# Zeros beside the last part's sums, attention products and sums one step behind the scores, and another order of the network steps

## The chip, the cores and the metric

The kernel runs on one core of a Trainium2 chip. The metric is device time in microseconds (us) of one execution, the median of several runs. A profile of one execution stands beside them: every instruction of the engines, and the transfers. TensorE is PE in it (its weight loads PEld), VectorE DVE, ScalarE ACT, GpSimd POOL, SyncE SP. PE, DVE and ACT compute; POOL issues the gathers here; SP issues most other transfers. Each engine works through its own instructions in order, and waits on semaphores for the others.

## The reference

Four layers over 3125 nodes of 256 features and 50000 edges sorted by destination, each added to `x` after a layer norm:

```python
# 1: relational graph layer, 16 relations
transformed = jnp.einsum('ni,rio->rno', h, weight)
out = segment_sum(transformed[rel_type, src] * norm, dst)
# 2: 16 experts, top 2, silu(x w1) * (x w2), then w3
# 3: two attention layers over the same edges, 8 heads of 32
h = (x @ W).reshape(N, HEADS, HEAD_DIM)
e = leaky_relu(alpha_s[src] + alpha_d[dst], 0.2)
ex = jnp.exp(e - segment_max(e, dst)[dst])
alpha = ex / (segment_sum(ex, dst)[dst] + 1e-16)
out = segment_sum(h[src] * alpha[:, :, None], dst) + b
# 4: a shared network of three layers, plus 4 expert networks of three
#    layers, the best 2 of them weighted by a softmax over their gates
return shared + gated
```

The first attention layer ends in an elu and feeds the second.

## The kernel before

Nodes lie in 25 tiles of 125 (`T` tiles of `R` rows), `x` in `xr`. The kernel goes through its stages one after the other.

**The relational layer.** `half_of_table` (L1251) multiplies half of the 16 weight matrices with one tile of normalized nodes (PE, L1266), copies the product to the buffer `tr` (ACT, L1269; two buffers) and writes 1 MB to a table in DRAM (SP, L1273). The loop over `n` runs 50 such halves. Between them stand the other engines' work in a written order: the layer norms of the next tiles (DVE and ACT, L104), edge records (n = 2), their placing into source order (`placing`, n = 10 and 11), the sending of places (`sending`, from n = 12), and from `n == 2 * S0[1]` on the gathers of table rows by the edges (POOL, L113) and their sums by destination (PE, L985, with one-hot matrices from DVE). Source nodes are in three parts (`S0 = (0, 7, 15)`), so that sums of the first two parts run while later halves are made; `a0`, `a1` set how fast `part_summed` is taken. The records for placing go out to `recs` and come back through loads that POOL issues (L1079).

**The last part's sums and the routing.** The loop over `items` (25 of them, one per tile) gathers and sums the third part, finishes a tile, and makes its expert logits. `blank` (L1356) fills the slots `xs` of the experts' inputs with zeros, 1 MB at a time from a row of zeros in SBUF, eleven transfers on SP in all; later the nodes are scattered into these slots by POOL. `blank` depends on nothing but the zeros. The loop's order on PE, DVE, ACT and SP is written by hand (`manual_schedule`), while what the zeros of `xs` wait for leaves them free to be issued earlier.

**The experts** (`pieces`): slots of 256 rows, PE-bound, and then the way back to the nodes.

**The attention layers.** `layer` (L1908) runs steps s = −1 to 25 with four tiles in hand: `new` (s+1), `now` (s), `old` (s−1), `older` (s−2). For a tile, `fetch` gathers 17 rows of 128 edges into three buffers `g0`, `g1`, `g2` (6, 6 and 5 chunks; three buffers each), `scans` finds running maxima (DVE L1824, L1825, after ACT's copies L1821), `one_hot` makes the destination matrix `oh` (DVE L1837), `carried` joins maxima over partitions (DVE L1842 to L1848, PE L1851), `lookup` and `destinations` bring the destination's term (PE L1880, DVE L1833), `scores` makes `z = exp(...)` (DVE, ACT L1866), `weighted` multiplies each gathered row by `z` (DVE L1886, one call for each of the three parts), `summed` adds up by destination (PE L1894) and `means` divides (DVE L1900 to L1906). Before, `weighted(now, 0..2)` and `summed(now, 0..1)` stand in the tile's own step, after its scores, and `summed(old, 2)` in the next. `tail1` to `tail4` are what follows `means`: for layer 1 the elu, a transpose, the product with the next layer's weights and the write of the next table.

A gather into a buffer waits for the sum that last read it:

```python
                    if len(added[k]) >= 3:
                        after_all(rows[0], [added[k][-3]])
```

**The networks** run inside layer 2, on pairs of tiles. `residual` is layer 2's `tail1`; `normalize`, `first_layers`, `gates`, `second_layers`, `choice`, `shares`, `spread`, `shared_out`, `third_layers` and `finish` are called from three places in a step, each with a lag in steps from the pair's second `residual` (`due`); a lag that is even falls on even steps and an odd one on odd steps:

```python
            def slot(s):
                run(s, (1, first_layers), (2, second_layers), (2, spread), (4, third_layers))
            def mid(s):
                run(s, (4, finish), (1, gates))
            def end(s):
                run(s, (2, shared_out), (0, normalize), (1, choice), (1, shares))
```

`slot` stands after `scores`, `mid` and `end` at the end of the step. `last` does the remaining pairs after the last step. `sel` and `sel_lt`, two small constants of the networks, are set up by POOL's iota (L2052) and DVE (L2054 to L2056); in the trace this work lies in layer 1.

Of the kernel before, what the change touches and what calls it, by code (L numbers as in the profile page):

```python
# [17 lines left out]
T = 25  # L18
# [5 lines left out]
H = 8  # L24
# [21 lines left out]
def gnn_kernel(ctx: ExitStack, tc: tile.TileContext, a: dict, out: bass.AP):  # L46
# [834 lines left out]
    def by_tiles(ctx, start_i, hard):  # L881
# [120 lines left out]
        with ExitStack() as mk:  # L1002
# [279 lines left out]
            with tc.manual_schedule():  # L1282
# [5 lines left out]
                for t in range(T):  # L1288
                    for half in range(2):
# [16 lines left out]
                        if n == 2:  # L1306
                            edge_records(sp, *loaded)
                            short.close()
                            sp = short.enter_context(tc.tile_pool(name="places_t", bufs=1))
                            placing = places(sp, *edges_of_tiles(sp))  # L1310
                        elif n == 10:
                            take_one(placing)
                        elif n == 11:
                            take_one(placing)
                            take_one(placing)
                            short.close()
                            sp = short.enter_context(tc.tile_pool(name="sent_t", bufs=1))
                            sending = sent(sp)
                        elif n > 11:
                            take_one(sending)  # L1320
                            take_one(sending)

                        if n == 2 * S0[1]:
                            for r in rels[:3]:
                                for k in range(2):
                                    fetch(r, k)
                                    if r.n == 0:
                                        hot(r, k)
                        a0, a1 = 2 * S0[1] + 1, 2 * S0[2] + 1
# [18 lines left out]
        with ExitStack() as st:  # L1348
# [7 lines left out]
            def blank(k, c0, c1):  # L1356

                nc.sync.dma_start(xs[k][c0 * SL:c1 * SL, :].rearrange("(p a) f -> p a f", p=128),
                                  zero[:, None, :].to_broadcast([128, (c1 - c0) * SL // 128, D]))
# [348 lines left out]
            with tc.manual_schedule(engines={ET.PE, ET.DVE, ET.Activation, ET.SP}):  # L1708
                slot_steps = pieces()
                route = routing(batches[0])  # L1710
                for s, w in enumerate(items):
                    if 1 <= s < 12:
                        k, c = (0, 4 * (s - 1)) if s < 6 else (1, 4 * (s - 6))
                        blank(k, c, min(c + 4, USED[k]))
# [47 lines left out]
        with ExitStack() as st:  # L1762
# [4 lines left out]
            fx = fixed.tile([128, 128 + D], F32, name="fx")  # L1767
            iota_ps, bias_ps = fx[:, :R], fx[:R, 128:]
            nc.vector.tensor_copy(iota_ps, iota_r[:, :R])
# [3 lines left out]
            def hidden(wx, xT):  # L1773
                p = ps.tile([R, D + 2 * H], F32, name="p_x")
                for k in range(2):
                    nc.tensor.matmul(p, xT[:, k, :], wx[:, k, :], start=(k == 0), stop=(k == 1))  # L1776
                return p
# [18 lines left out]
            def fetch(w):  # L1796
                w.g = []
                for k, (i0, i1) in enumerate(PARTS):
                    g = pool.tile([128, i1 - i0, DX], F32, name=f"g{k}", bufs=3)
                    rows = [gather(g[:, i - i0, :], w.h_tab, src_i[:, w.t, i:i + 1]) for i in range(i0, i1)]  # L1800

                    if len(added[k]) >= 3:
                        after_all(rows[0], [added[k][-3]])
                    w.g.append(g)
# [48 lines left out]
            def scores(w):  # L1853
# [11 lines left out]
                w.z = ad_e.rearrange("q h i -> q (h i)").rearrange("q (i h) -> q i h", h=H)  # L1865
# [22 lines left out]
            def summed(w, k):  # L1888

                if k == 0:  # L1890
                    w.p = ps.tile([R, DX], F32, name="p_sum")
# [16 lines left out]
            def layer(h_tab, ad, bias, tail1, tail2, tail3, tail4, slot=None, mid=None, end=None, last=None):  # L1908
# [7 lines left out]
                for s in range(-1, T + 1):  # L1916
# [9 lines left out]

                    if now:
                        one_hot(now)
                        destinations(now)
                    if older and s < T:  # L1930
                        tail4(older)
                    if now:
                        carried(now)
                    if old:
                        summed(old, 2)
# [6 lines left out]
                    if now:  # L1942
                        weighted(now, 0)
                    if old:
                        means(old)
                        tail1(old)
                        tail2(old)
                        tail3(old)
                    if now:
                        summed(now, 0)  # L1950
                        weighted(now, 1)
                        summed(now, 1)
                        weighted(now, 2)
                    if s == T:
                        tail4(older)
                        tail4(old)
                    if mid and now:
                        mid(s)
# [5 lines left out]
            def transposed(x):  # L1964
                p = ps.tile([128, 2, R], F32, name="p_x")
# [120 lines left out]

            def first_layers(u):
                n = u.n * R
                xT = pool.tile([128, 2, 2 * R], F32, name="xT2", bufs=2)
                for i in range(u.n):  # L2090
                    nc.scalar.copy(xT[:, :, i * R:(i + 1) * R], transposed(u.xc[:, i, :]))
                u.h1 = pool.tile([128, 2, 2 * R], F32, name="sh1")
                u.g1 = pool.tile([128, n_e, 2 * R], F32, name="eh1")
                for w, dst, bias in ([(s1[:, :, m * 128:(m + 1) * 128], u.h1[:, m, :n], b1[:, m:m + 1])
                                      for m in range(2)] +
                                     [(e1[:, e], u.g1[:, e, :n], eb1[:, e:e + 1]) for e in range(n_e)]):
                    p = ps.tile([128, 2 * R], F32, name="p_x")
                    for k in range(2):
                        nc.tensor.matmul(p[:, :n], w[:, k, :], xT[:, k, :n], start=(k == 0), stop=(k == 1))  # L2099
                    relu(dst, p[:, :n], bias)  # L2100
                u.pg = ps.tile([R, 2, n_e], F32, name="p_x")
# [14 lines left out]
            def second_layers(u):  # L2116
# [3 lines left out]
                p = ps.tile([128, 2 * R], F32, name="p_x")  # L2120
                for k in range(2):
                    nc.tensor.matmul(p[:, :n], s2[:, k, :], u.h1[:, k, :n], start=(k == 0), stop=(k == 1))
                relu(u.h2[:, :n], p[:, :n], b2)
                for half in range(2):
                    p = ps.tile([128, 2 * R], F32, name="p_x")
                    for k in range(2):
                        nc.tensor.matmul(p[:, :n], e2[:, 2 * half + k, :], u.g1[:, 2 * half + k, :n],
                                         start=(k == 0), stop=(k == 1))
                    relu(u.g2[:, half, :n], p[:, :n], eb2[:, half:half + 1])
# [44 lines left out]
            def spread(u):  # L2174
                n = u.n * R
                p = ps.tile([n_e + 1, 2 * R], F32, name="p_x")
# [4 lines left out]
                u.pw = ps.tile([128, 2, 2 * R], F32, name="p_x")  # L2181
# [7 lines left out]
            def third_layers(u):  # L2189
                u.po = ps.tile([R, 2, D], F32, name="p_x")  # L2190
# [21 lines left out]

            def slot(s):
                run(s, (1, first_layers), (2, second_layers), (2, spread), (4, third_layers))

            def mid(s):
                run(s, (4, finish), (1, gates))

            def end(s):
                run(s, (2, shared_out), (0, normalize), (1, choice), (1, shares))  # L2220

            def last():

                u, v, w = pairs[-3:]
                for step, p in ((third_layers, u), (finish, u), (first_layers, v), (normalize, w), (gates, v),
                                (second_layers, v), (choice, v), (shares, v), (first_layers, w), (gates, w),
# [5 lines left out]
            with tc.manual_schedule():  # L2232
                layer(tabs[1], ads[1], biases[1], residual, *[lambda w: None] * 3, slot, mid, end, last)
# [43 lines left out]
```

## Time and profile before

Seven runs took 2641.51 us in the median (2630.93 to 2648.55). The profiled execution took 2639.61 us, of which the span of the instructions is 2637.9.

| stage | from | to (us of the span) |
|---|---|---|
| relational table, sums of two parts | 0 | 670 |
| last part's sums, routing, scatters | 670 | 830 |
| experts, way back | 830 | 1433 |
| attention layer 1 (gathers 1433.6 to 1970.0) | 1433 | 1970 |
| hand-over | 1970 | 2014 |
| attention layer 2 and networks (gathers 2013.7 to 2548.9) | 2014 | 2549 |
| after the last gather | 2549 | 2638 |

The page gives busy time, share of the span and instructions of each engine, and the span in 40 slices of some 66 us. A digit is the busy share of a slice in tenths; `PEclk` is the clock granted to TensorE in tenths of full speed, and `DMA` the busy share of the 16 transfer engines:

```profile
PE 1964.2 (74%) x8604; PEld 1432.9 (54%) x8604; DVE 1370.0 (52%) x2950; ACT 800.3 (30%) x1699; POOL 1399.5 (53%) x1445
...
PE   5667879999564999997975266656653578888888
...
DVE  4068863322451441132114477777763687877783
...
POOL 1106555775677704120015777777763777777740
PEclk9788989999776999998995588888876788999898
DMA  6524434554336747674534555555552554444430
```

The first slice shows transfers at six tenths, POOL at one tenth and DVE at four; PE is near full in the middle of the table and in the experts (slices 13 to 20), and POOL at seven tenths through the attention layers, where the time between two gathers is not counted as busy.

A line of the profile's groups names line, engine, operation, `out<-in` and the number of instructions, then busy time and mean ns of one, then idle time before them with what ended it. A wait reads "engine tile line <- what it waited for: us in total, times, longest". In a timeline a row is start, length, engine, line, operation, shapes and the count of instructions in the group, and in brackets the idle time before it and its releaser.

### The profile page before, as it was taken

The page shows a single profiled execution, that of the slowest core. Times are in us where ns is not written, and L with a number is a line of the kernel's source. Part 1 is how long each engine was busy: PE and PEld are TensorE (multiplying, and loading weights), DVE is VectorE, ACT ScalarE, POOL GpSimd, SP SyncE. Part 2 cuts the span into 40 slices and gives each one's busy share as a digit, 9 for nine tenths or more (in the row PEclk, how much of TensorE's full clock was granted, in tenths as well). Part 3 has the DMA queues.
Part 4 walks back from the last instruction along what each step waited for, and adds up shares of the span by engine and source line. Part 5 has one row for each costly group of instructions (what it writes and reads, how often), then busy time and mean ns, then how long its engine had stood idle before and what let it go on. Part 6 is the DMA issues. An engine that isn't in the chain of part 4 may idle for free.

```text
span 2637.9 us, 26960 instructions
## 1 busy us (share of the span) xinstructions
PE 1964.2 (74%) x8604; PEld 1432.9 (54%) x8604; DVE 1370.0 (52%) x2950; ACT 800.3 (30%) x1699; POOL 1399.5 (53%) x1445
## 2 busy tenths in 40 slices
PE   5667879999564999997975266656653578888888
PEld 2234545555443878886862144444442466666665
DVE  4068863322451441132114477777763687877783
ACT  2221112222021242242223233333331344454542
POOL 1106555775677704120015777777763777777740
PEclk9788989999776999998995588888876788999898
DMA  6524434554336747674534555555552554444430
GB/s 215 207 96 141 135 117 162 200 190 167 106 104 196 232 127 249 197 213 135 192 108 114 151 139 144 146 139 140 139 138 53 136 131 138 140 136 141 135 92 15
DMA packets 192309, 386.35 MB, mean 146 GB/s; under 512 B 39900, under 2 KB 112588, under 8 KB 186659
## 3 DMA queue, kind: packets, MB, share of 16 engines
q0 software_dynamic: 76464, 189.38, 26.7%
q1 hardware_dynamic: 104543, 184.41, 20.6%
q10 hardware_dynamic: 11152, 10.75, 1.2%
q8 instruction: 71, 1.16, 0.2%
q14 instruction: 79, 0.65, 0.1%
HBM read 294.45 MB, written 89.87 MB: 146 GB/s over the span
## 4 chain that ended last, share of the span: by engine, by line
PE 48%; DVE 17%; DMA 10%; POOL 10%; issue 9%; ACT 5%; SPq 0%; ACTq 0%; POOLq 0%; DVEq 0%
PE ph L1574 10%; PE p_tr L1266 9%; POOL g L113 9%; PE p_sum L1894 7%; PE sum L985 5%; PE py L1584 5%; DMA table_t<-tr 4%; PE p_x L2099 3%; DMA g<-h_tab_t,src_t 2%; DVE oh L1837 2%; DMA g<-table_t,rg_t 2%; DVE g L1886 2%; PE p_x L2196 2%; PE p_x L1776 1%; DVE to_lane L1165 1%
## 5 line engine op out<-in xcount | busy, mean ns | idle before, releaser
L113 POOL DMA_INDIRECT g<-h_tab_t,src_t x850 | 810.5, 954 | 323.4 <-issue 266.7
L113 POOL DMA_INDIRECT g<-table_t,rg_t x450 | 448.4, 996 | 339.6 <-issue 115.5
L1894 PE MATMUL p_sum<-g,oh 128*125 128x264 f32 x1700 | 472.1, 439 | 14.3 <-DVE g L1886 11.7
L1894 PEld LDWEIGHTS p_sum<-g,oh 128*125 128x125 f32 x1700 | 362.0, 217 | 98.1 <-DVE g L1886 12.1
L1266 PE MATMUL p_tr<-w_rel_t,xT_t 128*125 128x512 f32 x800 | 371.7, 619 | 43.2 <-ACT tr L1269 43.2
L1574 PE MATMUL ph<-xcT,w 128*128 128x256 f32 x1312 | 310.1, 384 | 0.7 <-ACT xcT L1566 0.7
L985 PE MATMUL sum<-g,oh 128*125 128x256 f32 x900 | 243.1, 423 | 63.3 <-DMA g<-table_t,rg_t 33.1
L1266 PEld LDWEIGHTS p_tr<-w_rel_t,xT_t 128*125 128x125 f32 x800 | 155.7, 197 | 233.0 <-issue 177.2
L1886 DVE TENSOR_TENSOR g<-g,p_e 128x1536 f32<-128x1536 f32 x150 | 244.9, 1661 | 47.0 <-ACT g L1868 28.3
L1574 PEld LDWEIGHTS ph<-xcT,w 128*128 128x128 f32 x1312 | 248.9, 193 | 34.2 <-ACT xcT L1566 1.1
L1578 DVE TENSOR_TENSOR hT<-silu,ph 128x256 f32<-128x256 f32 x164 | 68.8, 421 | 376.7 <-ACT silu L1577 376.6
L1269 ACT COPY tr<-p_tr 125x512 f32<-125x512 f32 x200 | 115.2, 587 | 486.9 <-PE p_tr L1266 400.2
L985 PEld LDWEIGHTS sum<-g,oh 128*125 128x125 f32 x900 | 184.6, 210 | 111.7 <-issue 56.5
L113 POOL DMA_INDIRECT y<-ys,pos_i x50 | 61.4, 1228 | 327.3 <-DMA ys<-yc 297.6
L1000 DVE TENSOR_TENSOR xr<-xr,sum 125x256 f32<-125x256 f32 x75 | 31.4, 418 | 245.4 <-PE sum L985 202.3
L1584 PE MATMUL py<-w,hT 128*128 128x256 f32 x656 | 155.4, 380 | 0.2 <-DVE hT L1578 0.2
L1577 ACT ACTIVATE silu<-ph 128x256 f32<-128x256 f32 x164 | 62.9, 384 | 237.0 <-PE ph L1574 236.9
L1584 PEld LDWEIGHTS py<-w,hT 128*128 128x128 f32 x656 | 123.6, 190 | 16.9 <-DVE hT L1578 0.6
L1967 PE MATMUL p_x<-ident,en 125*128 125x125 f32 x50 | 16.7, 436 | 143.9 <-DVE en L1996 143.9
L1837 DVE TENSOR_TENSOR oh<-lo_t,fx 128x2125 f32<-128x2125 f32 x50 | 117.2, 2343 | 0.0
L1873 ACT ACTIVATE rows<-rows,minus_p 125x2176 bf16<-125x2176 bf16 x50 | 105.2, 2105 | 26.3 <-DMA g<-h_tab_t,src_t 17.7
L1866 ACT ACTIVATE p_e<-es 128x136 f32<-128x136 f32 x50 | 14.4, 287 | 322.4 <-DVE es L1864 322.4
(341 smaller groups left out, 2473.9 us busy)
## 6 DMA issues: line engine op xcount, KB each, us to landing
w<-in_L_ffn_w SPq DMA_DIRECT2D x123, 512.0 KB
table_t<-tr SPq DMA_DIRECT2D x44, 1000.0 KB
rows<-lo_rows_t SPq DMA_DIRECT2D x50, 531.2 KB
g<-h_tab_t,src_t POOLq DMA_INDIRECT x850, 2.9
xc<-xs_t SPq DMA_DIRECT2D x41, 256.0 KB
ys<-yc ACTq DMA_DIRECT2D x41, 256.0 KB
xs_t<-zero SPq DMA_DIRECT2D x9, 1024.0 KB
g<-table_t,rg_t POOLq DMA_INDIRECT x450, 5.5
```

The lines of the kernel that those rows point to most:

```text
L113: return nc.gpsimd.indirect_dma_start(out=dst, out_offset=None, in_=table, in_offset=bass.IndirectOffsetOnAxis(ap=idx, axis=0))
L985: m = nc.tensor.matmul(r.p[:R, :D], r.oh[k][:, i - i0, :], r.g[k][:, i - i0, :], start=(i == r.parts[0][0]), stop=(i == r.parts[1][1] - 1))
L1266: m = nc.tensor.matmul(p, xT[:, k, t * R:(t + 1) * R], w_rel[:, k, r0:r0 + 2, :].rearrange("p r o -> p (r o)"), start=(k == 0), stop=(k == 1))
L1269: nc.scalar.copy(tr[:, 2 * q * D:(2 * q + 2) * D], p)
L1574: nc.tensor.matmul(p[:, which, :], u.w12[:, which, k, m * 128:(m + 1) * 128], u.xcT[:, k, :], start=(k == 0), stop=(k == 1))
L1578: nc.vector.tensor_mul(u.hT[:, m, :], s, p[:, 1, :])
L1584: nc.tensor.matmul(u.py[:, j, :], u.hT[:, m, j * 128:(j + 1) * 128], u.w3[:, m, :], start=(m == 0), stop=(m == nh - 1))
L1837: nc.vector.tensor_tensor(w.oh, lo[:, w.t, :, None].to_broadcast([128, CT, R]), iota_ps[:, None, :].to_broadcast([128, CT, R]), OP.is_equal)
L1873: nc.scalar.activation(w.rows, w.rows, AF.Abs, bias=minus_p[:R, :])
L1886: nc.vector.tensor_mul(g, g, w.z[:, i0:i1, :, None].to_broadcast([128, i1 - i0, H, HD]))
L1894: m = nc.tensor.matmul(w.p, w.oh[:, i, :], w.g[k][:, i - i0, :], start=(i == 0), stop=(i == CT - 1))
L2099: nc.tensor.matmul(p[:, :n], w[:, k, :], xT[:, k, :n], start=(k == 0), stop=(k == 1))
```

## The change

Three things move, and two layouts go with them. The zeros each wait for the last sum so far, so they can't be issued before the last part's sums, and begin at item 0 instead of 1. In the relational loop the placing, the sending and the first gathers stand one half or two later. In the attention layers `weighted` and `summed` of a tile move to the next step, between the `one_hot` of the tile that follows and its scores; `tail3` comes to the front of a step, `destinations` behind the sums, `tail4` behind `tail1`. The networks' steps are called from the front (`early`), before the scores (`fill`), after them (`slot`) and at the end; `turned`, the two transposes of a pair, becomes a step of its own.

```diff
-                        elif n == 10:
+                        elif n == 11:
                             take_one(placing)
-                        elif n == 11:
+                        elif n == 12:
...
-                        elif n > 11:
+                        elif n > 12:
...
-                        if n == 2 * S0[1]:
+                        if n == 2 * S0[1] + 2:
...
-                        a0, a1 = 2 * S0[1] + 1, 2 * S0[2] + 1
+                        a0, a1 = 2 * S0[1] + 2, 2 * S0[2] + 1
...
-                nc.sync.dma_start(xs[k][c0 * SL:c1 * SL, :].rearrange("(p a) f -> p a f", p=128),
-                                  zero[:, None, :].to_broadcast([128, (c1 - c0) * SL // 128, D]))
+                fill = nc.sync.dma_start(xs[k][c0 * SL:c1 * SL, :].rearrange("(p a) f -> p a f", p=128),
+                                         zero[:, None, :].to_broadcast([128, (c1 - c0) * SL // 128, D]))
+                after_all(fill, [sums_of[-1]])
...
-                    if 1 <= s < 12:
-                        k, c = (0, 4 * (s - 1)) if s < 6 else (1, 4 * (s - 6))
+                    if s < 11:
+                        k, c = (0, 4 * s) if s < 5 else (1, 4 * (s - 5))
```

In the attention layers, the layout in PSUM (`fx` holds the row numbers in bf16, the bias and now `z`; `p_x` has three banks and `p_sum` one) and the step:

```diff
-            fx = fixed.tile([128, 128 + D], F32, name="fx")
-            iota_ps, bias_ps = fx[:, :R], fx[:R, 128:]
-            nc.vector.tensor_copy(iota_ps, iota_r[:, :R])
+            fx = fixed.tile([128, 64 + D + CT * H], F32, name="fx")
+            iota_ps, bias_ps = fx[:, :64].bitcast(BF16)[:, :R], fx[:R, 64:64 + D]
+            z_ps = fx[:, 64 + D:].rearrange("q (i h) -> q i h", h=H)
...
-                    if len(added[k]) >= 3:
-                        after_all(rows[0], [added[k][-3]])
+                    if w.t >= 3:
+                        after_all(rows[0], [added[k][w.t - 3]])
...
+                    if older:
+                        tail3(older)
+                    if early:
+                        early(s)
                     if now:
                         one_hot(now)
-                        destinations(now)
-                    if older and s < T:
-                        tail4(older)
+                    if old:
+                        weighted(old, 0)
+                        summed(old, 0)
                     if now:
                         carried(now)
                     if old:
-                        summed(old, 2)
+                        for k in (1, 2):
+                            weighted(old, k)
+                            summed(old, k)
+                    if now:
+                        destinations(now)
+                    if fill:
+                        fill(s)
                     if new:
                         lookup(new)
                     if now:
                         scores(now)
                     if slot and now:
                         slot(s)
-                    if now:
-                        weighted(now, 0)
                     if old:
                         means(old)
                         tail1(old)
+                    if older:
+                        tail4(older)
+                    if old:
                         tail2(old)
+                    if s == T:
                         tail3(old)
-                    if now:
-                        summed(now, 0)
-                        weighted(now, 1)
-                        summed(now, 1)
-                        weighted(now, 2)
-                    if s == T:
-                        tail4(older)
                         tail4(old)
-                    if mid and now:
-                        mid(s)
                     if end and now:
                         end(s)
```

And the networks, where `first_layers` and `second_layers` also put two products into one tile of PSUM before the activations read them:

```diff
+            def turned(u):
+                n = u.n * R
+                p = ps.tile([128, 2, 2 * R], F32, name="p_x", bufs=3)
+                for i in range(u.n):
+                    for k in range(2):
+                        nc.tensor.transpose(p[:, k, i * R:(i + 1) * R], u.xc[:, i, k * 128:(k + 1) * 128], ident[:R, :R])
+                u.xT = pool.tile([128, 2, 2 * R], F32, name="xT2", bufs=2)
+                nc.scalar.copy(u.xT[:, :, :n], p[:, :, :n])
...
+            def early(s):
+                run(s, (2, gates), (3, shared_out), (5, finish), (1, turned), (2, second_layers), (4, third_layers))
+
+            def fill(s):
+                run(s, (2, choice), (2, shares))
+
             def slot(s):
-                run(s, (1, first_layers), (2, second_layers), (2, spread), (4, third_layers))
-
-            def mid(s):
-                run(s, (4, finish), (1, gates))
+                run(s, (1, first_layers), (2, spread))
 
             def end(s):
-                run(s, (2, shared_out), (0, normalize), (1, choice), (1, shares))
+                run(s, (0, normalize))
```

`last` calls `turned` ahead of each of its two `first_layers`; the rest of it is as before.

## The prediction

> **What bounds the kernel now.** I read the page first, then busy times by stage, then the waits of the two stretches that the change touches, then the chain and single rows in layer 2.
>
> ```profile
> span 2637.9 us, 26960 instructions
> ...
> q10 hardware_dynamic: 11152, 10.75, 1.2%
> ...
> xs_t<-zero SPq DMA_DIRECT2D x9, 1024.0 KB
> ```
>
> The zeros are 10.75 MB on a queue of their own. The next view gives, for a stretch, its length, the busy time of PE, PEld, DVE, ACT and POOL, the granted clock, the DMA share and GB/s.
>
> ```profile
> 20.00:55.00 35.00, 23.40 (x58) 9.93 (x57) 25.17 (x49) 9.61 (x23) 2.99 (x8) 0.90 0.69 232
> 55.00:116.00 61.00, 31.43 (x60) 12.56 (x59) 4.10 (x6) 10.15 (x24) 14.29 (x26) 0.75 0.62 214
> 116.00:160.00 44.00, 28.80 (x69) 13.01 (x67) 10.29 (x18) 10.33 (x24) 0.00 (x0) 0.81 0.32 127
> ...
> 670.00:830.00 160.00, 74.55 (x256) 56.51 (x256) 53.30 (x140) 22.82 (x62) 122.03 (x123) 0.69 0.39 111
> ...
> 1433.00:1970.00 537.00, 298.34 (x1483) 225.21 (x1483) 359.19 (x704) 175.28 (x334) 406.90 (x426) 0.79 0.56 144
> ```
>
> No engine is full between 20 and 160; the transfers are (214 to 232 GB/s). In 670 to 830 and in layer 1 the bound is POOL, which issues gathers back to back (a gather each 1.25 us, 17 per tile: 21.3 us). Waits of 20 to 150:
>
> ```profile
> DVE ln_st L104 <- ACT ln_sq L103: 96.3, 3, 67.6
> ACT tr L1269 <- DMA table_t<-tr: 78.6, 9, 16.2
> ```
>
> ACT waits 78.6 us for table writes to free `tr`, and VectorE's normalization waits behind it on ACT. In layer 2 the chain of waits names PE and DVE in turn; one odd and one even step of it:
>
> ```profile
> 2412.47 2.34 DVE oh L1837
> ...
> 2417.00 3.91 PE p_sum L1894 x10
> 2420.91 0.41 PE p_ad L1880 x17
> 2421.63 0.65 ACT xT L2091 x2
> 2422.32 5.34 PE p_x L2099 x24
> ...
> 2439.28 3.51 PE p_sum L1894 x10
> 2442.80 0.45 PE p_ad L1880 x17
> 2443.24 1.32 PE p_x L2122 x4
> 2444.56 1.70 PE p_x L2127 x8
> ...
> 2448.15 4.24 PE p_x L2196 x16
> 2452.41 0.69 DVE xr L2200
> ```
>
> The scan L1824 starts at 2411.64, 2433.97 and 2455.69: steps of 22.33 and 21.72. From tile 27 (2079.55) to tile 49 (2566.72) there are 22 steps, 487.2 us, 22.14 each, against POOL's 21.3: the lag behind the last gather grows from 2.2 to 17.9 us. So layer 2 is set by this PE/DVE/ACT loop, not by POOL.
>
> **The change, part by part.** The profiled execution took 2639.61 (span plus 1.7), 1.9 below the median of the runs; the sum starts there.
>
> *Zeros, and the placing one half later.* Half 1's last copy L1269 ends at 25.9, half 10's at 146.5: nine halves in 120.6, 13.4 each. Without zeros a half costs (write + filling)/2 with its two buffers. A write takes 13.3 to 16 in the later halves; filling is four copies spaced by their eight matmuls, about 4: 8.7 to 10, I take 9.1. Half 10 then ends at 25.9 + 82 = 108. The records for placing are loaded by POOL (L1079, 59.8 to 101.9, landing 5.6 later), so placing cannot start before 107.5; it started at 150.35, and I expect 113: −37 (−31 to −42). From there to n=25 a half takes some 15 us of VectorE, then PE sets the pace (108 of 112 us busy in 448 to 560). Placing from n=11 instead of 10 means that one more half lies done in the time that transfers set, and one fewer (6.9 us) in PE's: −7 (−8 to 0). Together **−44** (−50 to −31) at the first gather of part 3 (670.7).
>
> The eleven fills now wait on SP, each for the last sum of the item before it. Behind them on SP stand the slot and weight loads (791), needed after the last fill. They run beside part 3's gathers: 105 GB/s plus 1 MB per item of 8.7 us (120 GB/s) is 225, and the stretch 20 to 55 shows 232. So nearly all fits: **+3** (0 to +15, the upper end if landing slips by 1.3 us in each of the eleven).
>
> [...]
>
> *Layer 1: products and sums one step later.* L1886 and L1894 of a tile move into the next step. Busy DVE work per step is 359/25 = 14.4, PE 12: POOL stays the bound. But the buffers of tile 3 come free one step later. At 1481.7 DVE stood 18.7 us at L2054, which waits for POOL's iota queued behind 51 gathers; its step resumed at 1500.3. POOL's gathers of tile 3 begin at 1500.2; they would now wait for tile 0's products and sums in that late step, some 9 us (one_hot 2.33, product 1.75, sums 3.9). **+8** (0 if the iota lands elsewhere, +10). The hand-over to layer 2 has the same work, with one tile's sums more behind the last scores: **+2** (−2 to +8).
>
> *Layer 2, odd step* (`turned`, `shared_out`, `finish` at the front; `first_layers` late), from the scan: scans .83, `shared_out` .66, `finish` .60, `one_hot` 2.26 (start to start), the product of part 0 1.6: 5.95. PE has then been idle over 3 us, and the sums start. What idling costs is seen here:
>
> ```profile
> 2549.59 0.38 PE L1851 MATMUL p_c<-ident,cin 8*128 8x8 f32 x2 [2.22 <-DVE cin L1847]
> ...
> 2549.90 4.06 PE L1894 MATMUL p_sum<-g,oh 128*125 128x264 f32 x10
> ...
> 2541.23 5.61 PE L1894 MATMUL p_sum<-g,oh 128*125 128x264 f32 x24
> ```
>
> Ten matmuls after 2.22 us of idling took 406 ns each; 24 without idling 234 each. The twelve of part 0 so take 4.6 to 4.9, I take 4.6; the transposes .3, parts 1 and 2 2.8 and 2.3 at 234 ns: 16.0. Lookup .6, `first_layers` 24 × .21 = 5.0: 21.7. Its last activations .9, the residual's two ACT passes 1.06, the copies L1821 .6: the next scan at **24.3**, 22.5 if PE stays fast. ACT works in order, so those copies stand behind all six activations; before, L1886 and `choice` filled DVE there.
>
> [...]
>
> *Even step* (`gates`, `second_layers`, `third_layers` at the front, `choice` and `shares` in the middle, `normalize` late). DVE is the loop: scans .83, `gates` .37, `one_hot` 2.26, the products 1.6 + 1.57 + 1.4, `carried` 1.41, the reduction L1833 .49, `choice` and `shares` 4.15, `scores` 3.08, `means` 1.34, the residual 1.09: 19.6, each from start to start in before's rows. Then comes what two products (3.15) and PE hid before: residual's ACT 1.06, the table load 1.28, square root .2, reciprocal and scaling 1.2, copies .6: 4.3. Next scan at **23.9**.
>
> A pair of steps is 48.2 against 44.28 (2 × 22.14): +3.95. The first pair of tiles has no networks behind it yet, so ten pairs: **+40** (+21 with fast PE, +50 with a microsecond more in each odd step). The wider `p_x` (three banks) and `first_layers` by twos save nothing: its 24 matmuls are PE-bound (5.34). The one-hot against a bf16 row in PSUM costs the same (its rows: 1.1 ns an element in either form). Table loads stay 12 and 12.
>
> *After the last scan*: the last sums and `choice` stand before the rest: **+3** (0 to +6).
>
> Sum: −44 + 3 + 8 + 2 + 40 + 3 = **+12**: 2651.6, by the median's 1.9 **2653**.
>
> **Rivals.**
> *A, the other side: the zeros' gain stays whole and layer 2 stays fast.* If PE's matmuls hold 234 ns in odd steps, layer 2 costs +21, and if POOL's iota is passed, layer 1 costs 0: −44 + 3 + 0 + 2 + 21 + 3 = −15: **2627**. It decides from a layer 2 step of 23.2 or less (then its +23 less 44 wins). For it: the 24-matmul rows; against: every ten-matmul row after a PE wait.
> *B, the zeros bound nothing.* If table writes land no faster (ACT's waits stay) or the records' loads slip, the gain is 20: 2653 + 24 = **2677**. For it: 127 GB/s with still 4 to 6 us waits in 116 to 160 after the last zero.
> *C, the loop falls under POOL's pace.* DVE's own work is some 19 us a step. If `normalize` and the activations hide, layer 2 takes 21.3 a step: 22 × .84 = −18 in place of +40: **2595**. Against it: ACT in order before L1821.
> *D, zeros collide with the gathers*, +15 for +3: **2665**.
>
> **How the numbers follow.** Forecast .50, A .20, B .12, C .10, D .08. About 0.3% (8 us) can be told from no change: 2633.6 to 2649.4. The forecast gives slower .40, same .10; A faster .16, same .04; B slower .12; C faster .10; D slower .08. Faster .26, same .14, slower .60. The forecast's own range is 2636 to 2672; to hold 8 in 10 with A, D and most of B: 2615 to 2682 (C is left out).
>
> **What would show it.** After: the rows `xs_t<-zero` near 625 to 725; ACT's wait for table writes halved; placing near 113 and part 3's first gather near 627. Gathers of tile 3 waiting for sums of PE. Scans of layer 2 spaced 24.3 and 23.9, the twelve first sums above .35 us each, POOL waiting for sums near the end. I am wrong if the scans are spaced 21.4 (C), or part 3 starts after 645 (B).

## The result and the profile after

The changed kernel takes 2662.6 us in the median of 18 runs, the kernel before 2638.3 in 46 runs beside them: a ratio of 1.0091 (95% interval 1.0079 to 1.0103), slower by 24 us. Forecast were 2653 us, slower, in a range of 2615 to 2682; that was 12 us above the 2641.5 of the kernel before that the forecast started from, so the direction came true and the measured step is twice as large. The profiled execution's span went from 2637.9 to 2656.9. From the first gather of each stage in the two traces:

| stretch | before | after | difference | forecast |
|---|---|---|---|---|
| start to part 3's first gather | 670.72 | 645.06 | −25.7 | −44 |
| to layer 1's first gather (1433.61, 1410.84) | 762.9 | 765.8 | +2.9 | +3 |
| to layer 2's first gather (2013.71, 1993.14) | 580.1 | 582.3 | +2.2 | +10 |
| to the scan of tile 27 (2079.55, 2059.06) | 65.8 | 65.9 | +0.1 | 0 |
| 22 steps to the scan of tile 49 (2566.72, 2582.01) | 487.2 | 523.0 | +35.8 | +40 |
| to the end of the span | 71.2 | 74.9 | +3.7 | +3 |
| sum | 2637.9 | 2656.9 | +19.0 | +12 |

The stretches of the front, in the same columns as before (length; busy time of PE, PEld, DVE, ACT, POOL; clock; DMA share; GB/s):

```profile
20.00:55.00 35.00, 25.24 (x58) 10.86 (x57) 25.14 (x49) 9.45 (x23) 3.72 (x9) 0.85 0.45 154
55.00:116.00 61.00, 53.88 (x125) 22.72 (x124) 4.10 (x6) 20.16 (x47) 14.32 (x26) 0.97 0.39 146
...
670.00:830.00 160.00, 83.03 (x329) 67.26 (x328) 59.13 (x150) 29.86 (x78) 122.41 (x124) 0.74 0.63 197
```

Between 55 and 116 PE does 125 matmuls where it did 60; the zeros are gone from there. They are now issued from 638.1 to 737.9; between 670 and 830, 111 GB/s became 197, and POOL's busy time is the same 122.4 us (122.0). ACT's wait for the table writes, from 20 to 150:

```profile
DVE ln_st L104 <- ACT ln_sq L103: 63.0, 3, 47.9
ACT tr L1269 <- DMA table_t<-tr: 48.2, 10, 9.8
```

78.6 us of waiting are 48.2 now, and none of these waits is above 9.8. In layer 2 the chain of waits over an odd step and the beginning of an even one:

```profile
2415.27 0.63 DVE eh L2206
2415.90 0.60 DVE xr L2219
2416.50 2.28 DVE oh L1841
2418.78 1.67 DVE g L1890
2420.49 4.93 PE p_sum L1898 x12
2425.42 0.22 PE p_c L1855 x2
2425.64 5.09 PE p_sum L1898 x22
2430.73 0.41 PE p_ad L1884 x17
2431.14 5.19 PE p_x L2116 x24
2436.36 0.83 ACT eh L2093 x2
2437.19 0.40 ACT ln_xc L2081
2438.20 0.43 ACT es L1825 x2
2438.66 0.45 DVE fw L1828
```

The scans start at 2414.42, 2438.66 and 2462.20: 24.24 for the odd step, 23.54 for the even one. This is one serial chain: DVE makes `oh` and the first product, PE sums all 34 matmuls, looks up, and does the first layers, and ACT's last activations and the residual come before the three copies that the next scan needs. The timeline has the twelve slow sums, the wait of VectorE at the odd step's end, and the uncovered normalization at the even one's:

```profile
2420.49 4.93 PE L1898 MATMUL p_sum<-g,oh 128*125 128x264 f32 x12 [3.45 <-DVE g L1890]
...
2438.66 0.44 DVE L1828 TENSOR_TENSOR_SCAN fw<-cut_ft,es 128x136 f32<-128x136 bf16 x1 [5.40 <-ACT es L1825]
...
2446.71 2.94 PE L1898 MATMUL p_sum<-g,oh 128*125 128x264 f32 x12
...
2459.02 1.28 ACT L2087 ACT_TABLE_LOAD   x1
...
2460.55 0.17 DVE L2088 RECIPROCAL ln_st<-ln_st 125x2 f32<-125x2 f32 x1 [1.35 <-ACT ln_st L2087]
2460.75 0.91 ACT L2090 ACTIVATE ln_xc<-ln_xc,ln_st 125x256 f32<-125x256 f32 x2 [0.23 <-DVE ln_st L2088]
2461.57 0.60 ACT L1825 COPY es<-g 128x48 f32<-128x48 f32 x3
```

The same twelve sums take 4.93 us after PE idled 3.45 us, and 2.94 in the even step, where the second and third layers keep PE busy ahead of them, from 2439.24 on. The granted clock (the figure behind POOL's count) shows what differs:

```profile
2407.50:2410.91 3.41, 1.42 (x10) 0.69 (x6) 2.37 (x8) 1.61 (x7) 2.68 (x3) 1.00 0.39 104
2410.91:2424.56 13.65, 6.11 (x17) 4.13 (x18) 10.41 (x14) 8.99 (x13) 9.74 (x11) 0.50 0.56 139
2424.56:2458.69 34.13, 30.68 (x172) 24.13 (x170) 23.67 (x66) 11.60 (x30) 22.80 (x24) 1.00 0.45 121
```

Nearly all of the slow sums lie in a stretch at half clock (0.50, 13.65 us long), the even step's in one at full clock (1.00, 34.13 us). The half clock begins 9.6 us ahead of the first slow sum, behind 3.41 us in which PE still worked 1.42 us.

### The profile page after: what moved, and what is told of

The parts are those of the page before. It is cut to its first block, busy times and chain, and to the rows that moved or that the text cites. A ratio compares the mean times of both kernels' runs of the same rounds, so it can differ in the third digit from the quotient of the medians.

```text
span 2656.9 us, 27198 instructions
## 1 busy us (share of the span) xinstructions
PE 1976.5 (74%) x8608; PEld 1435.8 (54%) x8608; DVE 1362.7 (51%) x2951; ACT 787.0 (30%) x1688; POOL 1402.8 (53%) x1445
## 5 line engine op out<-in xcount | busy, mean ns | idle before, releaser
L1890 DVE TENSOR_TENSOR g<-g,fx 128x1536 f32<-128x1536 f32 x150 | 243.8, 1650 | 0.1
L1832 PE MATMUL p_c<-ident,fw 128*8 128x128 f32 x100 | 26.9, 366 | 167.3 <-DVE fw L1828 167.3
L1870 ACT ACTIVATE fx<-es 128x136 f32<-128x136 f32 x50 | 14.4, 287 | 401.4 <-DVE es L1868 397.4
```

The costliest lines, as they stand in the source:

```text
L1890: nc.vector.tensor_mul(g, g, w.z[:, i0:i1, :, None].to_broadcast([128, i1 - i0, H, HD]))
```

## The experiments

Each ratio is to the kernel before on the same chip, with its 95% interval.

### The front part alone

To the kernel before, of the change only this:

```diff
+                after_all(fill, [sums_of[-1]])
...
-                    if 1 <= s < 12:
-                        k, c = (0, 4 * (s - 1)) if s < 6 else (1, 4 * (s - 6))
+                    if s < 11:
+                        k, c = (0, 4 * s) if s < 5 else (1, 4 * (s - 5))
...
-                        elif n == 10:
+                        elif n == 11:
...
-                        if n == 2 * S0[1]:
+                        if n == 2 * S0[1] + 2:
-                        a0, a1 = 2 * S0[1] + 1, 2 * S0[2] + 1
+                        a0, a1 = 2 * S0[1] + 2, 2 * S0[2] + 1
```

> The kernel before with the relational loop's new indices and the zeros that wait, the attention layers and networks left as they were. My theory: the front part gains what the trace of the changed kernel shows at layer 1's first gather (1433.6 to 1410.8), whatever the rest is, so the time is 22 to 24 us under before: about 2616, and layer 2's steps stay at 22.1. Rival: the two halves of the change lean on each other (layer 1 starts earlier but on a colder PE or on fuller queues); then the gain is under 12 us, above 2626.

2605.4 us, 0.9898 (0.9867 to 0.9929). The front's gain stands by itself: part 3's first gather at 643.44, layer 1's at 1408.94. That is 24.7 us of the 30. Of the rest, layer 2's 22 steps took 21.66 each here and 22.14 in the one trace of before, some 10 us that one trace of each can't explain. I had expected 22 to 24 us, so the size was somewhat off; the rival, a gain under 12 us because the two halves of the change lean on each other, fell. This kernel is faster than both.

### The products back in their own step

To the changed kernel:

```diff
-                    if old:
-                        weighted(old, 0)
-                        summed(old, 0)
...
-                        for k in (1, 2):
-                            weighted(old, k)
-                            summed(old, k)
+                        summed(old, 2)
...
+                    if now:
+                        weighted(now, 0)
                     if old:
                         means(old)
...
+                    if now:
+                        summed(now, 0)
+                        weighted(now, 1)
+                        summed(now, 1)
+                        weighted(now, 2)
```

> The changed kernel with the attention products and sums put back into the tile's own step, the networks in their new order. My theory: it is the late products that cost, because they leave the first layers' activations and the normalization without cover at a step's end, while the networks' new order takes the second and third layers off PE's queue behind the lookup. Then VectorE's work of an even step is some 20 us and of an odd one under 20, PE fits, POOL's 21.4 sets layer 2's steps, and the time is about 2612 (35 to 50 us under the changed kernel). Rival: the networks' order itself costs; then the steps stay at 22.5 or more and the time is above 2640.

2614.3 us, 0.9932 (0.9909 to 0.9956): 42 us under the changed kernel, by the two ratios. The steps of layer 2 are 21.96 in the mean, in pairs of 19.1 and 25.3. So taking the late products out gives back all that layer 2 had lost. But the pair, 44.4, is that of before (44.3): the networks' new order gains nothing there, and POOL's pace, which I expected, isn't reached. The odd step's ten sums now are the slow ones:

```profile
2435.01 0.38 PE L1855 MATMUL p_c<-ident,cin 8*128 8x8 f32 x2 [3.74 <-DVE cin L1851]
2435.32 4.76 PE L1898 MATMUL p_sum<-g,oh 128*125 128x264 f32 x10
```

They take 476 ns each, after 3.74 us of idling.

### The networks back in their order of before

To the changed kernel:

```diff
             def slot(s):
-                run(s, (1, first_layers), (2, spread))
+                run(s, (1, first_layers), (2, second_layers), (2, spread), (4, third_layers))
             def end(s):
-                run(s, (0, normalize))
+                run(s, (4, finish), (1, gates), (2, shared_out), (0, normalize), (1, choice), (1, shares))
```

`turned` is called by `first_layers` again, and `early` and `fill` are gone.

> The changed kernel with the networks' steps in their order of before (first, second and third layers and spread after the scores; the rest at the end), the products still late. My theory (late products cost, the networks' new order makes some of it good): even steps have second layers, spread and third layers (8 us of PE) behind the lookup again, odd steps have gates and choice behind the first layers: steps above 25 us, and the time is above 2680. Rival (the networks' order costs): steps of 22.5 or less, under 2630.

2752.8 us, 1.0457 (1.0425 to 1.0490). Its steps are 27.4 to 29.2 from tile 30 on. With late products the old order costs a further 97 us, by the two ratios; the reason, as the order is written and not tried by itself, is that all of the networks' PE work stands behind the lookup, which stands behind all 34 sums. So the networks' new order belongs to the late products; it repairs most of what they would cost, and not all.

### The next tile's copies ahead of the networks' activations

To the changed kernel:

```diff
+            def taken(w):
+                w.es = pool.tile([128, 2, H, CT], F32, name="es", bufs=2)
+                for g, (i0, i1) in zip(w.g, PARTS):
+                    nc.scalar.copy(w.es[:, 0, :, i0:i1], heads(g[:, :, D:]))
...
                     if now:
                         scores(now)
+                    if slot and now and new:
+                        taken(new)
                     if slot and now:
                         slot(s)
```

> The changed kernel with the next tile's three copies (the input of the scans) put before the first layers' activations on ScalarE in layer 2. My theory: the odd step ends on ScalarE's order (scans wait 5.4 us for these copies behind six activations and the residual), so odd steps lose 4 to 5 us and even ones 1 to 1.5; a pair goes from 47.8 to POOL's 42.8 or a little over, and the time falls by 40 to 65 us, to 2600 to 2620. Rival: PE sets the odd step (its sums on a slow clock, then the first layers); then the scans only move ahead and wait later, and the time falls by less than 15 us.

2621.3 us, 0.9951 (0.9933 to 0.9968), against the changed kernel's 1.0091: 37 us less, just short of the lower end. The steps are now 25.8 and 18.6, together 44.4 in place of 47.8. The wait of 5.4 us is gone, which shows ScalarE's order at the odd step's end as its price. What keeps the pair from 42.8 the waits suggest: the slow sums remain, and `gates` now waits for the first layers instead:

```profile
PE p_sum L1902 <- DVE g L1894: 31.1, 9, 3.5
DVE gm L2134 <- PE p_x L2130: 33.7, 9, 3.8
```

These are waits from 2150 to 2550 (total, times, longest): nine odd steps, 3.5 us of PE idle ahead of the sums in each as before, and 3.7 us of VectorE at `gates`.

### Four kernels on a chip that paused

The next four ran on a chip where the kernel before took 3312 us itself. In every trace of that lot engines stand still for some 10 us in most steps from about 440 us on. ACT has the most of it: 38 to 54 waits of over 5 us each whose releaser the profile gives as "remote", where it finds no instruction or transfer of this core; the traces of before and after have no such wait. One line of `zeros_alone`:

```profile
ACT xT L2002 <- remote: 249.3, 22, 13.7
```

PE then waits for ACT. Their ratios are not used; what lies ahead of the pauses, or within a run of PE work, is. `zeros_alone` and `pe_kept_busy` are shown further down, where they ran again; the other two put the copies of the experiment above into the front part alone and into the kernel with the products back.

> The kernel before with only the zeros that wait for the last part's sums, all indices of the relational loop as before. The recorded step says that placing one half later is worth 7 us (one half fewer in PE's stretch). My theory now: it is worth nothing, as VectorE reaches the placing behind the layer norm at 116.5 either way, and the sums' chain sets the rest; then the first gather of part 3 starts at 640 to 647, as with the indices moved (645, 643), and the time is 24 to 30 us under before. Rival (the recorded step): the first gather at 650 or later and a gain of 17 to 20 us.

3286.4 us, 0.9923. Up to 440 us: placing at 119.99, first gather at 174.91, halves 14 to 31 all 29.8 to 30.1 us earlier than before.

> The changed kernel with sixteen more matmul instructions on PE at the front of an odd step, ahead of the transposes of a pair (their output is overwritten by these). Theory (PE's idle time makes the first sums slow): the twelve sums that follow take 2.9 us in place of 4.9, the odd step falls from 24.2 to 22.5 and the time by 15 to 20 us. Rival (the slow sums come of something else, such as waiting for their operands): the twelve still take 4.5 us or more, and the time stays or rises by up to 5 us.

3162.9 us, 0.9572. The twelve sums behind the added matmuls take 2.94 us in most odd steps.

> The front part alone, and the next tile's three copies ahead of the networks' work on ScalarE. Theory: in the order of before VectorE's scans wait 1.5 us for these copies in nearly every step of layer 2, so a pair of steps falls from 43.3 to POOL's 42.8 or a little over, the lag of 9 us at the last tile goes to under 5, and the time falls to 2595 to 2601 (front alone: 2605). Rival: PE and VectorE set the step otherwise, and the time stays within 4 us of 2605.

3299.9 us, 0.9961; nothing follows.

> The changed kernel with the products back in their own step and the three copies ahead of the networks' work. Theory: the pair of 44.4 loses 1.5 to 2 us at the end of the even step and 1.5 at the end of the odd one, which brings it to POOL's 42.8; the time falls from 2614 to 2590 to 2600. Rival: PE's slow sums after its 3.7 us of idling in the odd step (476 ns each) set the pair, and the time stays above 2608.

3023.6 us, 0.9134; nothing follows but that the pauses depend on the program.

### The zeros alone, again

The kernel before with the waiting zeros, all indices of the relational loop as before.

> The same kernel as zeros_alone, since PE paused for some 10 us a step in every kernel of that lot, the kernel before too (3312 us). Its trace up to 440 us, before the pauses begin, had the placing start at 120.0, the first gather at 174.9 and the halves 29.8 us earlier than before at n = 14 to 31, against 29.0 at n = 31 with the indices moved. So my theory: the moved indices are worth nothing or cost 2 to 4 us; the first gather of part 3 at 640 to 643 and 26 to 34 us under before (with the indices moved: 30 under). Rival (the recorded step): 650 or later, 17 to 23 us under before.

2611.1 us, 0.9893 (0.9848 to 0.9937), the same as with the indices moved (0.9898). Placing starts at 119.04, part 3's first gather at 640.78, 29.9 us before that of the kernel before. With the indices moved it stood at 645.06, 643.44, 643.73, 640.36, 648.23, 641.80 and 645.31 in seven kernels, and another kernel with only the zeros changed, further down, has it at 632.68. So moving the placing by a half is worth nothing; if it does anything, it costs.

### PE kept busy ahead of the first sums

To the changed kernel, in `turned`:

```diff
+                for _ in range(2):
+                    for i in range(u.n):
+                        for k in range(2):
+                            nc.tensor.matmul(p[:, k, i * R:(i + 1) * R], u.xc[:, i, k * 128:(k + 1) * 128],
+                                             ident[:R, :R], start=True, stop=True)
                 for i in range(u.n):
                     for k in range(2):
                         nc.tensor.transpose(p[:, k, i * R:(i + 1) * R], u.xc[:, i, k * 128:(k + 1) * 128], ident[:R, :R])
```

> The same kernel as pe_kept_busy. There the twelve first sums of an odd step took 2.94 us behind the added matmuls, on a PE that paused elsewhere. Theory: so here too, in place of 4.9; odd steps of 22.5 and a time 15 to 20 us under the changed kernel's 1.009 of before, that is 1.002 to 1.003 of it. Rival: slow in any case, or the time is taken back by the activations; 1.007 or more.

2649.5 us, 1.0046 (1.0023 to 1.0068): 12 us less than the changed kernel with more work on PE. The sums are fast and the odd step is 22.2 (22.2 to 22.4 from tile 36 on), where the forecast had 22.5 for a PE that stays fast:

```profile
2417.20 2.94 PE L1898 MATMUL p_sum<-g,oh 128*125 128x264 f32 x12 [1.08 <-DVE g L1890]
...
2435.97 3.18 PE L2150 MATMUL p_x<-eh,e 128*128 128x250 f32 x8
```

Part of it is lost again: in the even step the second layers' eight matmuls, 1.85 us in the changed kernel, take 2.4 to 3.3 in many steps, and the even step goes to 24.7 in these and 23.5 in the others. The slow stretch moved to another place, and the granted clock shows it:

```profile
2411.35:2414.76 3.41, 3.04 (x14) 2.36 (x15) 3.38 (x5) 3.38 (x2) 2.57 (x3) 0.50 0.47 119
2414.76:2431.83 17.07, 15.99 (x97) 13.63 (x97) 12.32 (x24) 5.35 (x14) 13.03 (x14) 1.00 0.63 156
2431.83:2435.24 3.41, 1.96 (x13) 1.34 (x13) 1.80 (x5) 3.38 (x8) 2.50 (x4) 1.00 0.33 100
2435.24:2438.66 3.42, 3.42 (x10) 2.79 (x9) 3.42 (x3) 2.58 (x4) 2.51 (x4) 0.50 0.50 125
```

The added matmuls run in the first of these rows (0.50), and the full clock is back at 2414.76, before the sums at 2417.20. It is halved again for the second layers, behind 3.41 us in which PE worked 1.96 us and never idled for more than 1.45.

### Copies ahead, with the products back and with the zeros alone

`taken` and its call, as above, in the kernel with the products back and in the one with the zeros alone:

```diff
+                    if slot and now and new:
+                        taken(new)
                     if slot and now:
                         slot(s)
```

> The same kernel as products_back_and_copies, whose lot ran on a chip that paused PE. Theory: the pair of 44.4 loses 3 us at its two ends and comes to POOL's 42.8; 2590 to 2600, 0.982 to 0.987 of before. Rival: PE's slow sums in the odd step hold the pair; 0.990 or more.

2606.9 us, 0.9892 (0.9858 to 0.9926), against 0.9932 without the copies moved. From tile 31 on the steps are 17.4 and 24.1 to 26.8, 42.8 a pair in the mean, which is POOL's pace: from 2150 to 2500 it idles 0.3 us ahead of a gather and never longer. So layer 2's loop has little more to give here. The forecast, 0.982 to 0.987, was missed by a little: the first pairs of layer 2 still take up to 47.0. The waits from 2150 to 2500 say the same of POOL's pace: ScalarE is now ahead of POOL, and the copies wait for gathers.

```profile
ACT es L1821 <- DMA g<-h_tab_t,src_t: 38.0, 10, 5.0
```

> The kernel before with the zeros that wait and the three copies ahead of the networks' work, indices and order of before. Theory: its steps of 22.2 lose the 1.5 us that the scans wait for the copies and come to POOL's 21.4; the lag of 20 us at the last tile goes under 6; 2592 to 2600, 0.982 to 0.986 of before (zeros alone: 0.989). Rival: PE is the loop in this order too (the first sums are slow after its wait, and the first layers follow) and the scans only wait elsewhere: 0.988 to 0.990.

2617.6 us, 0.9923 (0.9899 to 0.9947): not better than the zeros alone. In the order of before, the steps that end at tiles 29 and 31 became 32.4 and 28.9, and the mean from tile 27 is 22.55 a step (zeros alone: 22.22). In the longer of the two the copies wait for gathers, and the networks' transposed input, behind them in ScalarE's order, comes late to PE:

```profile
2084.09 0.26 ACT L1818 COPY es<-g 128x40 f32<-128x40 f32 x1 [4.40 <-DMA g<-h_tab_t,src_t]
2084.94 3.65 PE L2106 MATMUL p_x<-xT,s 128*128 128x250 f32 x8 [8.72 <-ACT xT L2098]
```

From tile 31 on the steps are 21.85 in the mean (zeros alone: 22.34). So the copies save half a microsecond a step there, and the two long steps take more than that away; no run removes them. PE still waits 39.9 us in 16 steps (2150 to 2500) for `cin`, with the slow sums behind it, which is what the rival named. The theory fell here, as POOL's 21.4 is not reached; the ratio lies above the rival's range of 0.988 to 0.990 too.

## Why the prediction was right, step by step

**Layer 2, +40: right in its path and nearly in its size.** The odd step was forecast at 24.3 and is 24.2, the even one at 23.9 and is 23.5; the sum was 36, as the steps grow to that only over the first five. Each reason was tried by itself. The late products are the cause: back in their step, the 22 steps take 483.0 us in place of 523.0. The odd step's end on ScalarE's order is worth 3.4 us a pair (copies ahead). The slow first sums are worth 2 us an odd step (PE kept busy), though part of that returns elsewhere. After shows slow sums behind 3.45 us of idling (411 ns each), and before behind 2.22 (406 ns); with PE kept busy, sums behind 1.08 us stayed fast (245 ns). The forecast of 24.3 rests on the row of before, and the sums came as slow as it has them. But the length of the last idling, by which I chose it, does not decide by itself: in the changed kernel 1.61 us of idling (from 2246.65) left the full clock as it was (1.00 from 2233.42 to 2267.55), while with PE kept busy the clock was halved after 1.45 at most. In the rows here the half clock followed 3.41 us in which PE had worked 1.42 us in the changed kernel, 1.96 us with PE kept busy and 1.19 us in before (2546.28 to 2549.69, ahead of the ten sums of the prediction; 0.50 from 2549.69 to 2553.10). Half and full clock last 13.65 and 34.13 us in the rows of the changed kernel, and a full one 17.07 with PE kept busy: 4, 10 and 5 times 3.41. In none of the three was PE idle for all of the 3.41 us; what decides, no run takes apart. So the price of the slow sums was right, and the reason that I gave for it only in part.

**The networks' order: not told apart.** I priced the two moves together. Apart, the old order with late products is 97 us worse, and the new order with products in their place is no better than before. So the change has one move that costs and one that only pays that back in part.

**The front, −44: the step that failed.** It gave −25.7, outside the −31 to −50 that I allowed. Three things were mis-sized. A half took 9.8 us and not 9.1 (half 10 ends at 114.5, I said 108), and the layer norm ahead of the placing adds 3.9 more: the placing starts at 118.3 and not 113, 5 of the 18 us. "One more half lies done in the time that transfers set, and one fewer in PE's", −7, is worth 0: the zeros alone gain as much. And the start of the placing is 32 us earlier, while part 3's first gather is 26 earlier: half 13 ends 51 us earlier than before, but from half 33 on the lead is 25 to 26.5. My reading, which no run takes apart, is that the halves and the sums are dealt out by fixed `n`, and a half that is done early only waits for the sums that stand behind it. The zeros alone lose 1.4 us there (31.3 to 29.9) and the moved indices 6.4 in their profile. I had also named a start of part 3 after 645 as the sign of rival B, that the zeros bound nothing. At 645.06 it is met by the letter, and the gain lies nearer to B's 20 than to my 44; but ACT's waits for table writes, which B wanted unchanged, fell from 78.6 to 48.2.

**Zeros beside part 3's sums, +3: right.** It is +2.9. In the 95 us from its first gather part 3 has 205 GB/s where it had 105, and POOL's busy time is 71.98 us against 71.83; the row of before, then that of after:

```profile
671.00:766.00 95.00, 56.73 (x194) 43.34 (x195) 33.25 (x79) 13.49 (x39) 71.83 (x77) 0.73 0.37 105
...
645.00:740.00 95.00, 56.60 (x195) 43.92 (x196) 32.40 (x77) 12.89 (x37) 71.98 (x76) 0.72 0.67 205
```

The +15 at the upper end, and in rival D, was an estimate of mine for landings that slip by 1.3 us in each of the eleven fills, and no run shows it. The traces show a stretch that is 2.9 us longer, with a POOL as busy as before and 205 GB/s, under the 232 that before had from 20 to 55.

**Layer 1, +8: too much.** It is +2.8 (the gathers take 539.2 us in place of 536.4). The wait for POOL's iota is there, but behind the first product:

```profile
1461.04 1.75 DVE L1890 TENSOR_TENSOR g<-g,fx 128x1536 f32<-128x1536 f32 x1
...
1462.89 5.61 PE L1898 MATMUL p_sum<-g,oh 128*125 128x264 f32 x12 [3.34 <-ACT ohT L1878]
...
1477.55 0.28 DVE L2062 TENSOR_SCALAR sel_lt<-sel 5x256 f32<-5x256 f32 x1 [13.91 <-POOL sel L2060]
```

Tile 0's first buffer is free by 1468.5, so tile 3's gathers start on time, and POOL only waits 1.4 us in tile 3 and 2.2 in tile 4, together about the 2.8. I had left the constant's place in VectorE's order as in the trace of before; new work in front of it moved it. The hand-over, +2, is −0.6, and the end, +3, is +3.7.

The two misses went in opposite ways, 18 us of front less and some 11 us of attention less, so the sum came within 7 us in the traces and within 10 in the medians. That it came so close is luck. The best kernels found are the front part alone (0.9898), the zeros alone (0.9893) and the changed kernel with the products back and the copies ahead (0.9892). Their intervals overlap.

## What to carry to other kernels

A transfer that needs nothing early, like filling with zeros, belongs in a stretch whose pace another engine sets; moving it out of a stretch that transfers set gave 1.1% by itself. Work taken out of a step's end to stand "one step behind" can take away the cover of whatever else ends the step (here VectorE's wait for the copies before a scan went from at most 1.5 us to 5.40 in the odd step shown): list what then lies bare on the engine whose copies start the next step. And changes that came together should be priced apart, since here one gained some 27 us and the other cost some 50.

## What the runs showed of the hardware that was not expected

The slow stretch of PE is not removed by keeping PE busy at the place where it hurts: with odd steps' sums at 245 ns, the even steps' second layers went from 231 ns to between 295 and 415 in many steps, in the step shown at half clock (0.50 from 2435.24 to 2438.66), although PE had idled at most 1.45 us at a time ahead of them. One chip took 3312 us for a kernel that took 2636 to 2642 in all other medians, by pauses of some 10 us, most of them waits of ACT that the profile puts down to "remote", while the duration of single instructions stayed the same in the kernel with the zeros alone (L1895's sums 439 ns in the mean there, L1894's 439 before); the cause stays open.
